# TensorE's transposes of x replaced by 32x32 block transposes on VectorE, with the delta made transposed, turned back, and added by GpSimd

## Chip, core and metric

The kernel runs on one core of a Trainium2 chip. The metric is the device time of one execution in microseconds (us), the median of several runs. Five engines with queues of their own take part: TensorE (PE; PEld is its weight load), VectorE (DVE), ScalarE (ACT), GpSimd (POOL) and SyncE (SP, which only issues transfers). Matmuls write PSUM. Everything is 32-bit float.

## What is computed

x is [8, 512, 2048]. A conditioning layer y = x W^T + b + 2 (x A_b) B_b, with a rank-16 adapter chosen per batch, feeds a layer with 8 experts of rank 16, of which each token takes the one with the largest router logit:

```python
base_out = jnp.einsum('bti,oi->bto', x, W) + b
A = lora_As[adapter_mapping]
Bm = lora_Bs[adapter_mapping]
lora_h = jnp.einsum('bti,bir->btr', x, A)
lora_out = jnp.einsum('btr,bro->bto', lora_h, Bm)
y = base_out + lora_out * 2.0
logits = jnp.einsum('bsd,ed->bse', y, route_w)
topk_v, topk_idx = jax.lax.top_k(logits, 1)
route_weight = one_hot(topk_idx[..., 0], 8) * topk_v
h = jnp.einsum('bsd,erd->bser', y, A_ffn)
wh = route_weight[..., None] * h
out = x + jnp.einsum('bser,eor->bso', wh, Bw)
```

## The kernel before

y is only read through 136 rows: 128 of the experts (8 times 16) and 8 of the router, gathered in `proj` (`pj` on chip). So the kernel folds W into them once, and y is never made: the heads of a token are hl = x (W^T proj + 2 A_b (B_b proj)) + bias proj.

First stage, the fold. W comes as eight slices of 256 columns over all 2048 rows (line 92, 2 MB each, SP's queue, three buffers), with the first tiles of x between them. For each block of 128 columns, 16 matmuls against `pj` are summed in PSUM (`pc`, line 150) and copied by ScalarE to `c_sb` (line 157). Between them come the bias row (`pb`, line 172) and the adapters, which GpSimd gathers (lines 128 and 135): `ad_b` is transposed on TensorE (line 163) and multiplied with `pj` (`pg`, line 189), and a masked copy per batch is kept in `gm`.

For each batch, `fold_adapter` makes m_b = c + 2 A_b (B_b proj): 16 matmuls of `ad_a` with `gm` over all 128 partitions (`pm`, line 217), and VectorE's adds to `c_sb` (line 224).

Token stage: 32 tiles of 128 tokens go through three stages, one tile apart. `stage_transpose` turns the tile's 16 blocks of 128x128 on TensorE (`pxT`, line 163), four to a PSUM bank, and ScalarE copies each bank to `xT` (line 164). `stage_route` multiplies xT with m_b (`ph`, line 243), and a chain of seven small VectorE instructions (lines 247 to 258) picks the expert and gives `wh`, the weighted heads. `stage_out` transposes wh (`pw`, line 269), ScalarE copies it (`whT`, line 271), and four matmuls of 512 columns with whT as the weights and `fb` (the experts' output matrices) moving give the delta in token order (`po`, line 274); VectorE adds each to the tile of x in place (line 275), and GpSimd's queue stores the tile (line 279, 1 MB, 128 partitions). SP's queue loads x six tiles ahead (line 86).

The order of each engine's work is the tile framework's scheduler's, within the dependences and the buffers of the pools. One f32 matmul appears in the profile as two matmul records; a transpose as one.

Of the kernel before, what the change touches and what calls it, by code (L numbers as in the profile page):

```python
# [9 lines left out]
F32 = mybir.dt.float32  # L10
# [8 lines left out]
def kernel(  # L19
# [12 lines left out]
    """out = x + ffn(cond(x)), both linear up to the choice of one expert.  # L32

    The FFN reads y = cond(x) through NP = E*R + E rows only (its A rows, then
    its router rows), gathered in proj [D, NP].  So the products are taken as
        hl = x @ (W^T proj + 2 A_b (B_b proj)) + bias @ proj
    with A_b, B_b the adapter of batch b: y itself is never needed.

      x [B, T, D]        itok [1, B]          w [DO, D]
      bias [128, DO/128], column c holds rows c*128...  # L40
      cond_a [SLOTS*R, D], cond_b [SLOTS*R, DO], row = slot*R + r
      proj [DO, NP]      ffn_b [E*R, D], row = e*R + r
    """
    nc = tc.nc
    P = 128
    B, T, D = x.shape
# [5 lines left out]
    NI = D // P  # L52
    NO = DO // P
    WS = 256
    NWS = D // WS
    TPB = T // P
    NT = B * TPB
    NN = D // 512
# [3 lines left out]
    wpool = ctx.enter_context(tc.tile_pool(name="wpool", bufs=3))  # L62
    xpool = ctx.enter_context(tc.tile_pool(name="xpool", bufs=6))
    xtpool = ctx.enter_context(tc.tile_pool(name="xtpool", bufs=2))
    mpool = ctx.enter_context(tc.tile_pool(name="mpool", bufs=2))
    small = ctx.enter_context(tc.tile_pool(name="small", bufs=3))
    ps_t = ctx.enter_context(tc.tile_pool(name="ps_t", bufs=2, space=bass.MemoryType.PSUM))
    ps_a = ctx.enter_context(tc.tile_pool(name="ps_a", bufs=3, space=bass.MemoryType.PSUM))
    ps_o = ctx.enter_context(tc.tile_pool(name="ps_o", bufs=3, space=bass.MemoryType.PSUM))

# [1 line left out]
    it_i = const.tile([P, B], I32, name="it_i")  # L72
    nc.gpsimd.dma_start(out=it_i, in_=itok.to_broadcast([P, B]))  # L73
    pj = const.tile([P, NO, NP], F32, name="pj")
    nc.scalar.dma_start(out=pj, in_=proj.rearrange("(c p) e -> p c e", p=P))
    bias_sb = const.tile([P, NO], F32, name="bias_sb")
    nc.scalar.dma_start(out=bias_sb, in_=bias)
    fb = const.tile([P, D], F32, name="fb")
    nc.scalar.dma_start(out=fb, in_=ffn_b)

    x_tiles = {}

    def load_x(t):
        xt = xpool.tile([P, D], F32, tag="x", name=f"x_{t}")
        b, k = divmod(t, TPB)
        nc.sync.dma_start(out=xt, in_=x[b, ts(k, P), :])
        x_tiles[t] = xt

    w_tiles = []
    for s in range(NWS):  # L90
        wt = wpool.tile([P, NO, WS], F32, tag="w", name=f"w_{s}")
        nc.sync.dma_start(
            out=wt, in_=w[:, ts(s, WS)].rearrange("(c p) i -> p c i", p=P)
        )
        w_tiles.append(wt)
        if s >= 2:
            load_x(s - 2)

# [1 line left out]
    ident = const.tile([P, P], F32, name="ident")  # L100
    make_identity(nc, ident)
    # own[p, b] = p - R*b, in [0, R) where row p = (b, r) belongs to batch b
# [9 lines left out]
    # rank[p, e] = E - e: the largest among equal logits is the first expert  # L112
# [14 lines left out]
    ad_b = const.tile([P, DO], F32, name="ad_b")  # L127
# [6 lines left out]
    ad_a = const.tile([P, D], F32, name="ad_a")  # L134
    nc.gpsimd.indirect_dma_start(  # L135
        out=ad_a,
# [3 lines left out]
    )  # L140

# [1 line left out]
    c_sb = const.tile([P, NI, NP], F32, name="c_sb")  # L143

    def fold_w(s):
        for k in range(WS // P):
            ic = s * (WS // P) + k
            pc = ps_a.tile([P, NP], F32, tag="acc", name=f"pc_{ic}")
            for oc in range(NO):
                nc.tensor.matmul(  # L150
                    pc,
                    w_tiles[s][:, oc, ts(k, P)],
                    pj[:, oc, :],
                    start=(oc == 0),
                    stop=(oc == NO - 1),
                )
            nc.scalar.copy(c_sb[:, ic, :], pc)  # L157

    def transpose_rows(dst, src, name, n):
        for g in range(n // 4):  # L160
            pt = ps_t.tile([P, 4, P], F32, tag="tr", name=f"{name}_{g}")
            for j in range(4):
                nc.tensor.transpose(pt[:, j, :], src[:, ts(4 * g + j, P)], ident)  # L163
            nc.scalar.copy(dst[:, 4 * g : 4 * g + 4, :], pt)  # L164

    for s in range(NWS - 2):
        fold_w(s)

    # bias @ proj on all partitions
    pb = ps_a.tile([1, NP], F32, tag="acc", name="pb")  # L170
    for oc in range(NO):
        nc.tensor.matmul(  # L172
            pb,
            bias_sb[:, oc : oc + 1],
            pj[:, oc, :],
            start=(oc == 0),
            stop=(oc == NO - 1),
        )
    c0 = const.tile([1, NP], F32, name="c0")
    nc.vector.tensor_copy(c0, pb)  # L180
    c0b = const.tile([P, NP], F32, name="c0b")
    nc.gpsimd.partition_broadcast(c0b, c0)  # L182

    # g[(b, r), e] = B_b proj, scaled, one masked copy per batch
    ad_bT = xtpool.tile([P, NO, P], F32, tag="xT", name="ad_bT")
    transpose_rows(ad_bT, ad_b, "pbT", NO)
    pg = ps_a.tile([P, NP], F32, tag="acc", name="pg")
    for oc in range(NO):
        nc.tensor.matmul(
            pg,  # L190
            ad_bT[:, oc, :],
            pj[:, oc, :],
            start=(oc == 0),
            stop=(oc == NO - 1),
        )
    g_sb = const.tile([P, NP], F32, name="g_sb")
    nc.vector.tensor_copy(g_sb, pg)
    gm = const.tile([P, B, NP], F32, name="gm")
    for b in range(B):
        nc.vector.tensor_scalar(  # L200
            gm[:, b, :], g_sb, mask[:, b : b + 1], COND_SCALING, ALU.mult, ALU.mult
        )

    for s in range(NWS - 2, NWS):
        fold_w(s)

# [1 line left out]
    m_tiles = {}  # L208
    GRP = 512 // NP

    def fold_adapter(b):
        m = mpool.tile([P, NI, NP], F32, tag="m", name=f"m_{b}")
        for i0 in range(0, NI, GRP):
            n = min(GRP, NI - i0)
            pm = ps_a.tile([P, GRP, NP], F32, tag="acc", name=f"pm_{b}_{i0}")
            for j in range(n):
                nc.tensor.matmul(  # L217
                    pm[:, j, :],
                    ad_a[:, ts(i0 + j, P)],
                    gm[:, b, :],  # L220
                    start=True,
                    stop=True,
                )
            nc.vector.tensor_tensor(  # L224
                m[:, i0 : i0 + n, :], c_sb[:, i0 : i0 + n, :], pm[:, :n, :], ALU.add
            )
        m_tiles[b] = m
# [54 lines left out]
    for t in range(NT + 2):  # L282
        if t < NT:
            stage_transpose(t)
# [56 lines left out]
```

## Time and profile before

| | |
|---|---|
| median of 3 runs (lowest, highest) | 433.1 us (432.74, 433.37) |
| span of the profiled execution, first to last instruction | 431.1 us |
| TensorE busy | 403.6 us, 94% of the span |
| VectorE, ScalarE, GpSimd busy | 163.4, 87.5, 21.4 us |
| transfers | 88.57 MB, mean 205 GB/s |

The profile has one execution. Its span is 2.0 us under the median. A row of the table of groups gives line, engine, operation, what is written and read, shape and count, then busy time in us and the mean of one in ns, and after the bar the idle time ahead of it with what ended it. A row of the table by stage gives a stretch, its length, the busy time of PE, PEld, DVE, ACT and POOL with counts, the granted clock of TensorE, the busy share of the transfer engines and GB/s. A row of the timeline gives start, duration, engine and line.

### The profile page before, as it was taken

How to read it: one execution, taken by the hardware profiler on the slowest of the kernel's cores; microseconds unless marked ns; L12 is line 12 of the kernel's file. 1: busy time of each engine (PE TensorE's matmuls, PEld its weight loads, DVE VectorE, ACT ScalarE, POOL GpSimd, SP SyncE). 2: the span in 40 equal slices, each digit the busy share in tenths (PEclk: the TensorE clock that was granted, in tenths of full speed). 3: DMA queues.
4: the chain of work that ended last, by engine and by line, in shares of the span. 5: the costliest groups of instructions: out<-in, count | busy, mean ns of one | idle time of the engine just before them, and what ended most of it. 6: DMA issues, size and time to landing. Idle time of an engine off the chain costs nothing.

```text
span 431.1 us, 6278 instructions
## 1 busy us (share of the span) xinstructions
PE 403.6 (94%) x2672; PEld 326.9 (76%) x2672; DVE 163.4 (38%) x420; ACT 87.5 (20%) x181; POOL 21.4 (5%) x44
## 2 busy tenths in 40 slices
PE   0589999999999999999999999999999999999993
PEld 0589998999777787779777877777787777777751
DVE  0100000121633453454554455544364336334562
ACT  1000011024222212312221222122303321322200
POOL 1200000000000000000000000000000000000000
PEclk9999999999999999999999999999999999999998
DMA  8999999100246553557265545554563565362224
GB/s 240 370 377 377 365 366 372 76 2 2 98 155 236 197 228 163 202 202 278 106 242 239 196 169 222 195 196 195 207 246 135 213 252 220 132 246 111 100 98 195
DMA packets 28429, 88.57 MB, mean 205 GB/s; under 512 B 1392, under 2 KB 19824, under 8 KB 19824
## 3 DMA queue, kind: packets, MB, share of 16 engines
q1 hardware_dynamic: 21120, 50.33, 33.3%
q0 software_dynamic: 4928, 35.66, 20.3%
q10 hardware_dynamic: 2352, 2.17, 1.6%
q8 instruction: 21, 0.34, 0.3%
q14 instruction: 8, 0.07, 0.0%
HBM read 54.60 MB, written 33.55 MB: 204 GB/s over the span
## 4 chain that ended last, share of the span: by engine, by line
issue 93%; POOL 4%; POOLq 0%; DVE 0%
POOL out_dram L279 4%; POOLq L279 0%; POOL ad_b L128 0%; POOL ad_a L135 0%; POOLq L337 0%; POOL c0b L182 0%; POOL ident masks.py:199 0%; POOL ident masks.py:197 0%; DVE it_f L122 0%; DVE row_f L124 0%; DVE rank L116 0%; DVE row_i L126 0%; DVE mask L111 0%; POOL it_i L73 0%; POOL own_i L104 0%
## 5 line engine op out<-in xcount | busy, mean ns | idle before, releaser
L243 PE MATMUL ph<-m,xT 128*128 128x136 f32 x1024 | 129.5, 279 | 0.0
L243 PEld LDWEIGHTS ph<-m,xT 128*128 128x128 f32 x1024 | 123.3, 190 | 0.5 <-issue 0.5
L274 PE MATMUL po<-fb,whT 128*128 128x512 f32 x256 | 118.4, 605 | 0.8 <-ACT whT L271 0.8
L164 ACT COPY xT<-pxT 128x512 f32<-128x512 f32 x128 | 71.2, 587 | 148.0 <-PE pxT L163 147.6
L275 DVE TENSOR_TENSOR x<-x,po 128x512 f32<-128x512 f32 x128 | 87.7, 685 | 13.4 <-PE po L274 12.3
L274 PEld LDWEIGHTS po<-fb,whT 128*128 128x128 f32 x256 | 46.0, 189 | 51.7 <-issue 27.7
L150 PE MATMUL pc<-pj,w 128*128 128x136 f32 x512 | 63.2, 286 | 18.4 <-DMA pj<-in_proj_dram 16.0
L150 PEld LDWEIGHTS pc<-pj,w 128*128 128x128 f32 x512 | 62.2, 196 | 19.1 <-DMA pj<-in_proj_dram 16.0
L163 PE MATMUL pxT<-ident,x 128*128 128x128 f32 x512 | 72.7, 277 | 0.9 <-ACT xT L164 0.2
L163 PEld LDWEIGHTS pxT<-ident,x 128*128 128x128 f32 x512 | 57.6, 140 | 19.8 <-issue 11.6
L247 DVE TENSOR_TENSOR hl<-ph,c0b 128x136 f32<-128x136 f32 x32 | 9.6, 300 | 151.0 <-PE ph L243 151.0
L279 POOL DMA_DIRECT2D out_dram<-x x32 | 17.2, 538 | 335.9 <-DVE x L275 335.9
L217 PEld LDWEIGHTS pm<-gm,ad_a 128*128 128x128 f32 x256 | 31.3, 190 | 3.3 <-issue 3.3
L217 PE MATMUL pm<-gm,ad_a 128*128 128x136 f32 x256 | 32.1, 279 | 0.0
L224 DVE TENSOR_TENSOR m<-c_sb,pm 128x408 f32<-128x408 f32 (+1 forms) x48 | 23.8, 529 | 15.6 <-PE pm L217 13.6
L271 ACT COPY whT<-pw 128x128 f32<-128x128 f32 x32 | 8.5, 265 | 101.2 <-PE pw L269 101.2
L180 DVE COPY c<-pb 1x136 f32<-1x136 f32 x1 | 0.3, 288 | 56.3 <-PE pb L172 56.3
L157 ACT COPY c_sb<-pc 128x136 f32<-128x136 f32 x16 | 4.4, 272 | 70.7 <-PE pc L150 70.7
L258 DVE TENSOR_TENSOR wh<-hl,rw 128x128 f32<-128x128 f32 x32 | 9.4, 293 | 1.1
L256 DVE TENSOR_SCALAR rw<-rank,win,top 128x8 f32<-128x8 f32 x32 | 9.3, 291 | 1.2
L269 PE MATMUL pw<-ident,wh 128*128 128x128 f32 x32 | 8.7, 273 | 0.0
L251 DVE TENSOR_SCALAR key<-hl,top 128x8 f32<-128x8 f32 x32 | 7.4, 231 | 1.1
(36 smaller groups left out, 49.8 us busy)
## 6 DMA issues: line engine op xcount, KB each, us to landing
x<-in_x_dram SPq DMA_DIRECT2D x32, 1024.0 KB, 4.8
out_dram<-x POOLq DMA_DIRECT2D x32, 1024.0 KB, 4.1
w<-in_w_dram SPq DMA_DIRECT2D x8, 2048.0 KB, 14.4
pj<-in_proj_dram ACTq DMA_DIRECT2D x1, 1088.0 KB, 15.2
fb<-in_ffn_b_dram ACTq DMA_DIRECT2D x1, 1024.0 KB, 13.1
bias_sb<-in_bias_dram ACTq DMA_DIRECT2D x1, 8.0 KB, 15.1
it_i<-in_itok_dram POOLq DMA_DIRECT2D x1, 4.0 KB, 6.3
ad_b<-in_cond_b_dram,row_i POOLq DMA_INDIRECT x1, 8.3
```

The lines of the kernel that those rows point to most:

```text
L150: nc.tensor.matmul(pc, w_tiles[s][:, oc, ts(k, P)], pj[:, oc, :], start=(oc == 0), stop=(oc == NO - 1),)
L163: nc.tensor.transpose(pt[:, j, :], src[:, ts(4 * g + j, P)], ident)
L164: nc.scalar.copy(dst[:, 4 * g : 4 * g + 4, :], pt)
L217: nc.tensor.matmul(pm[:, j, :], ad_a[:, ts(i0 + j, P)], gm[:, b, :], start=True, stop=True,)
L224: nc.vector.tensor_tensor(m[:, i0 : i0 + n, :], c_sb[:, i0 : i0 + n, :], pm[:, :n, :], ALU.add)
L243: nc.tensor.matmul(ph, xT[:, ic, :], m[:, ic, :], start=(ic == 0), stop=(ic == NI - 1))
L247: nc.vector.tensor_tensor(hl, ph, c0b, ALU.add)
L256: nc.vector.tensor_scalar(rw, rank, win, top, ALU.is_equal, ALU.mult)
L258: nc.vector.tensor_tensor(wh.rearrange("p (e r) -> p e r", r=R), hl[:, :ER].rearrange("p (e r) -> p e r", r=R), rw.unsqueeze(2).to_broadca ...
L274: nc.tensor.matmul(po, whT, fb[:, ts(n, 512)], start=True, stop=True)
L275: nc.vector.tensor_tensor(xt[:, ts(n, 512)], xt[:, ts(n, 512)], po, ALU.add)
L279: nc.gpsimd.dma_start(out=out[b, ts(k, P), :], in_=xt)
```

## The change

The tokens go in units of 256, in pairs of batches b and b+4. A unit of x lies on chip as [128, 8, 512]: partition (i, t) holds, for token t of each of eight groups of 32, the i-th quarter of the features. Each unit is loaded and stored in four pieces of 32 partitions, by SP and ScalarE in and by SP and GpSimd out. VectorE transposes it in 32x32 blocks straight from SBUF (`turn_x`), which leaves 128 features on the partitions and 128 tokens along each row; TensorE's transposes of x and ScalarE's copies of them go. `W`, `ad_a` and `fb` are put in the same order of features by copies (`chunked`) on ScalarE or GpSimd.

The heads and the choice of the expert stay. The delta is made with blocks of `fb` as weights and whT (256 tokens) moving, so it comes out with features on the partitions (`pd`); VectorE turns it back in 32x32 blocks from PSUM to `dl`, and GpSimd adds dl to x.

W comes in 16 row chunks of 1 MB; all of c is summed at once over the chunks in six PSUM banks. The first two chunks of pj are loaded ahead of the others. The adapters of two batches are folded together, each with the 64 partitions of its half. The order of instructions is that of the program (`manual_schedule`).

```diff
-    wpool = ctx.enter_context(tc.tile_pool(name="wpool", bufs=3))
-    xpool = ctx.enter_context(tc.tile_pool(name="xpool", bufs=6))
-    xtpool = ctx.enter_context(tc.tile_pool(name="xtpool", bufs=2))
...
+    DQ = D // NQ
+    U = 256
+    UPB = T // U
+    NU = B * UPB
+    TPU = U // P
+    NG = U // Q
+    GJ = 4
+    PH = P // 2
+    HB = B // 2
...
+    cpool = ctx.enter_context(tc.tile_pool(name="cpool", bufs=6))
+    rpool = ctx.enter_context(tc.tile_pool(name="rpool", bufs=4))
+    xpool = ctx.enter_context(tc.tile_pool(name="xpool", bufs=5))
+    dpool = ctx.enter_context(tc.tile_pool(name="dpool", bufs=2))
+    small = ctx.enter_context(tc.tile_pool(name="small", bufs=2))
+    ps_s = ctx.enter_context(tc.tile_pool(name="ps_s", bufs=2, space=bass.MemoryType.PSUM))
+    def chunked(copy, dst, src):
+        copy(
+            dst.rearrange("p j (i a) -> p j i a", a=Q),
+            src.rearrange("p (i j a) -> p j i a", i=NQ, a=Q),
+        )
+    ctx.enter_context(tc.manual_schedule())
...
+    def load_w(oc):
+        wt = rpool.tile([P, D], F32, tag="r", name=f"w_{oc}")
+        nc.sync.dma_start(out=wt, in_=w[ts(oc, P), :])
+        w_tiles.append(wt)
+    units = [UPB * (b + h * HB) + k for b in range(HB) for h in range(2) for k in range(UPB)]
+    x_tiles = {}
+    def rows_of(dram, u):
+        b, k = divmod(u, UPB)
+        return dram[b, ts(k, U), :].rearrange("(g t) (i d) -> i t g d", t=Q, i=NQ)
+    def load_x(u):
+        xt = xpool.tile([P, NG, DQ], F32, tag="x", name=f"x_{u}")
+        src = rows_of(x, u)
+        for i, eng in ((0, nc.sync), (2, nc.scalar), (1, nc.sync), (3, nc.scalar)):
+            eng.dma_start(out=xt[ts(i, Q)], in_=src[i])
+        x_tiles[u] = xt
+    nc.scalar.dma_start(out=pj[:, :2], in_=proj_v[:, :2])
+    load_w(0)
+    nc.scalar.dma_start(out=pj[:, 2:], in_=proj_v[:, 2:])
+    nc.scalar.dma_start(out=bias_sb, in_=bias)
+    for oc in range(1, 4):
+        load_w(oc)
...
+    raw = [xpool.tile([P, 2, D], F32, tag="x", name=f"raw_{k}") for k in range(2)]
+    ad_b = raw[0][:, 0, :]
...
+    ad_ar = raw[0][:, 1, :]
...
+    ad_a = const.tile([P, NJ, P], F32, name="ad_a")
+    chunked(nc.gpsimd.tensor_copy, ad_a, ad_ar)
...
+    c_sb = cpool.tile([P, NJ, NP], F32, tag="c", name="c_sb")
+    GRP = 512 // NP
+    groups = [(j0, min(GRP, NJ - j0)) for j0 in range(0, NJ, GRP)]
...
+    with tc.tile_pool(name="ps_c", bufs=len(groups), space=bass.MemoryType.PSUM) as ps_c:
+        pcs = [
+            ps_c.tile([P, GRP, NP], F32, tag="pc", name=f"pc_{j0}") for j0, n in groups
+        ]
+        def fold_w(oc):
+            wv = dpool.tile([P, NJ, P], F32, tag="d", name=f"wv_{oc}")
+            chunked(nc.scalar.copy, wv, w_tiles[oc])
+            for pc, (j0, n) in zip(pcs, groups):
+                for k in range(n):
+                    nc.tensor.matmul(
+                        pc[:, k, :],
+                        wv[:, j0 + k, :],
+                        pj[:, oc, :],
+                        start=(oc == 0 and k == 0),
+                        stop=(oc == NO - 1),
+                        skip_group_check=True,
+                    )
+                if oc == NO - 1:
+                    nc.scalar.copy(c_sb[:, j0 : j0 + n, :], pc[:, :n, :])
...
+        for oc in range(NO):
+            fold_w(oc)
+            if oc + 4 < NO:
+                load_w(oc + 4)
+            if oc == 2:
+                fbr = raw[1][:, 0, :]
+                nc.scalar.dma_start(out=fbr, in_=ffn_b)
+                chunked(nc.gpsimd.tensor_copy, fb, fbr)
+            if oc in (3, 6, 9):
+                load_x(units[oc // 3 - 1])
+            if oc == 7:
+                fold_bias()
+            if oc in (8, 9, 10, 11):
+                turn_adapters(oc - 8)
+            if oc == 12:
+                project_adapters()
+                load_x(units[3])
+    ps_m = ctx.enter_context(tc.tile_pool(name="ps_m", bufs=2, space=bass.MemoryType.PSUM))
+    ps_d = ctx.enter_context(tc.tile_pool(name="ps_d", bufs=2, space=bass.MemoryType.PSUM))
...
+    def fold_adapters(b):
+        pair = (b, b + HB)
+        for bb in pair:
+            m_tiles[bb] = cpool.tile([P, NJ, NP], F32, tag="c", name=f"m_{bb}")
+        for j0, n in groups:
+            pms = [
+                ps_m.tile([P, GRP, NP], F32, tag="m", name=f"pm_{bb}_{j0}") for bb in pair
+            ]
+            for k in range(n):
+                for h, bb in enumerate(pair):
+                    nc.tensor.matmul(
+                        pms[h][:, k, :],
+                        ad_a[ts(h, PH), j0 + k, :],
+                        gm[ts(h, PH), bb, :],
+                        start=True,
+                        stop=True,
+                    )
+            for h, bb in enumerate(pair):
+                nc.vector.tensor_tensor(
+                    m_tiles[bb][:, j0 : j0 + n, :],
+                    c_sb[:, j0 : j0 + n, :],
+                    pms[h][:, :n, :],
+                    ALU.add,
+                )
...
+    def turn_x(u, t):
+        xT = rpool.tile([P, NJ, P], F32, tag="r", name=f"xT_{u}_{t}")
+        nc.vector.transpose(
+            xT.rearrange("p j (g t) -> p g j t", t=Q),
+            x_tiles[u][:, ts(t, NQ), :].rearrange("p g (j a) -> p g j a", a=Q),
+        )
+        xT_tiles[u, t] = xT
+    def heads(u, t):
+        xT = xT_tiles.pop((u, t))
+        m = m_tiles[u // UPB]
+        ph = ps_s.tile([P, NP], F32, tag="s", name=f"ph_{u}_{t}")
+        for j in range(NJ):
+            nc.tensor.matmul(
+                ph, xT[:, j, :], m[:, j, :], start=(j == 0), stop=(j == NJ - 1)
+            )
...
+    def turn_heads(u):
+        pw = ps_s.tile([P, TPU, P], F32, tag="s", name=f"pw_{u}")
+        for t in range(TPU):
+            nc.tensor.transpose(pw[:, t, :], wh_tiles.pop((u, t)), ident)
+        whT = small.tile([P, U], F32, tag="whT", name=f"whT_{u}")
+        nc.scalar.copy(whT.rearrange("p (t q) -> p t q", q=P), pw)
+        whT_tiles[u] = whT
+    def delta(u, j0):
+        pd = ps_d.tile([P, GJ, U], F32, tag="d", name=f"pd_{u}_{j0}")
+        for k in range(GJ):
+            nc.tensor.matmul(pd[:, k, :], fb[:, j0 + k, :], whT_tiles[u], start=True, stop=True)
+        dl = dpool.tile([P, NG, GJ * Q], F32, tag="d", name=f"dl_{u}_{j0}")
+        nc.vector.transpose(
+            dl.rearrange("p g (k a) -> p k g a", a=Q),
+            pd.rearrange("p k (g t) -> p k g t", t=Q),
+        )
+        xs = x_tiles[u][:, :, ds(j0 * Q, GJ * Q)]
+        nc.gpsimd.tensor_tensor(xs, xs, dl, ALU.add)
+    def store(u):
+        xt = x_tiles.pop(u)
+        dst = rows_of(out, u)
+        for i, eng in ((0, nc.sync), (2, nc.gpsimd), (1, nc.sync), (3, nc.gpsimd)):
+            eng.dma_start(out=dst[i], in_=xt[ts(i, Q)])
+    fold_adapters(0)
+    for t in range(TPU):
+        turn_x(units[0], t)
+    for n in range(NU + 1):
+        u = units[n] if n < NU else None
+        v = units[n - 1] if n else None
+        w_ = units[n + 1] if n + 1 < NU else None
+        if u is not None:
+            heads(u, 0)
+        if v is not None:
+            delta(v, 0)
+            delta(v, GJ)
+        if w_ is not None:
+            turn_x(w_, 0)
+        if u is not None:
+            heads(u, 1)
+        if v is not None:
+            delta(v, 2 * GJ)
+            delta(v, 3 * GJ)
+            store(v)
+            if n + 3 < NU:
+                load_x(units[n + 3])
+        if w_ is not None:
+            turn_x(w_, 1)
+        if u is not None:
+            turn_heads(u)
+            if n % (2 * UPB) == 2 * UPB - 2 and n // (2 * UPB) + 1 < HB:
+                fold_adapters(n // (2 * UPB) + 1)
```

## The prediction

> **What bounds the kernel now.** I read the shares of busy time first, then the slices for clock and transfers, then the table by stage, the groups, and the timeline where a rate was needed.
>
> ```profile
> PE 403.6 (94%) x2672; PEld 326.9 (76%) x2672; DVE 163.4 (38%) x420; ACT 87.5 (20%) x181; POOL 21.4 (5%) x44
> ...
> PEclk9999999999999999999999999999999999999998
> ...
> GB/s 240 370 377 377 365 366 372 76 2 2 98 155 236 197 228 163 202 202 278 106 242 239 196 169 222 195 196 195 207 246 135 213 252 220 132 246 111 100 98 195
> ```
> ```profile
> 200.00:300.00 100.00, 99.84 (x627) 77.39 (x628) 47.01 (x120) 24.65 (x50) 4.78 (x9) 1.00 0.52 197
> ```
> TensorE is busy 94% of the span at full clock, and in the token stage (200 to 300 us) 99.84 of 100 us, while VectorE does 47, ScalarE 25, GpSimd 5 and the transfers run at half their share. So the token stage is as long as TensorE's list of instructions. In the first 75 us the transfers run at their top, 365 to 377 GB/s.
>
> ```profile
> L243 PE MATMUL ph<-m,xT 128*128 128x136 f32 x1024 | 129.5, 279 | 0.0
> L274 PE MATMUL po<-fb,whT 128*128 128x512 f32 x256 | 118.4, 605 | 0.8 <-ACT whT L271 0.8
> L164 ACT COPY xT<-pxT 128x512 f32<-128x512 f32 x128 | 71.2, 587 | 148.0 <-PE pxT L163 147.6
> L275 DVE TENSOR_TENSOR x<-x,po 128x512 f32<-128x512 f32 x128 | 87.7, 685 | 13.4 <-PE po L274 12.3
> L150 PE MATMUL pc<-pj,w 128*128 128x136 f32 x512 | 63.2, 286 | 18.4 <-DMA pj<-in_proj_dram 16.0
> L163 PE MATMUL pxT<-ident,x 128*128 128x128 f32 x512 | 72.7, 277 | 0.9 <-ACT xT L164 0.2
> L217 PE MATMUL pm<-gm,ad_a 128*128 128x136 f32 x256 | 32.1, 279 | 0.0
> L224 DVE TENSOR_TENSOR m<-c_sb,pm 128x408 f32<-128x408 f32 (+1 forms) x48 | 23.8, 529 | 15.6 <-PE pm L217 13.6
> ```
> The transposes of x are 72.7 us of TensorE, heads 129.5, the delta 118.4. Two records stand for one f32 product, one for a transpose. Means of single matmuls overlap, so I take the spacing from long runs:
>
> ```profile
> 75.78 14.99 PE L150 MATMUL pc<-pj,w 128*128 128x136 f32 x128
> ...
> 416.98 0.69 DVE L275 TENSOR_TENSOR x<-x,po 128x512 f32<-128x512 f32 x1 [0.16 <-PE po L274]
> ...
> 417.83 0.69 DVE L275 TENSOR_TENSOR x<-x,po 128x512 f32<-128x512 f32 x1
> ...
> 424.75 0.53 POOL L279 DMA_DIRECT2D out_dram<-x  x1 [3.69 <-DVE x L275]
> ```
> 128 records of 136 columns take 15.0 us: 0.116 us each. Two records of 512 columns are 0.85 apart: 0.43 each. A straight line gives 0.116 + 0.313*120/376 = 0.216 for 256 columns. From the last store's issue at 424.75 to the span's end at 431.1 is 6.4 us for 1 MB.
>
> **The change, part by part.** One iteration of the new loop is a unit of 256 tokens.
>
> TensorE per unit: heads 2*32*0.116 = 7.4; delta 16 products of 256 columns, 32*0.216 = 6.9 (the same columns, so no gain); two transposes of wh 0.3. Sum 14.6 us. Before, 256 tokens took two tiles of (423.7-94.2)/32 = 10.3, or 20.6. The 72.7 us of transposes is most of the difference. The adapter product has 64 rows per matmul in two row groups: 64 records a fold, 7.4 us if they run in turn, 3.7 if they pair; VectorE's 12 adds (10*0.577 + 2*0.29 = 6.4) and two buffers pace it either way, so I take 6.4 a fold.
>
> VectorE per unit loses eight adds of 0.685 and gains six block transposes. No transpose of VectorE is in the trace; the nearest rows are its adds: 128x512 in 0.685 and 128x408 in 0.577, that is 0.152 + N*1.04 ns. So 2048 elements take 2.29 and 1024 take 1.22. Lower bound: half the slope (1.2 and 0.7). Upper: twice the slope, if a 32-bit block is filled and emptied in turn (4.4 and 2.3). The row's slope is taken, since a transpose reads one stream where the add reads two. Per unit: 2*2.29 + 4*1.22 + two chains of small instructions at 1.81 (102.75 to 104.56 on the timeline) = 13.1 us, against TensorE's 14.6. Drawn out, it fits: transpose of x(t=1) ends 3.4 us into the next iteration, the next chain starts at 3.9. Slack is about 0.5 us, so anything that lengthens VectorE shows.
>
> GpSimd per unit: four adds of 1024. Nearest row: GpSimd's 128x128 select, 0.28 us, 2.2 ns an element, so 2.25 each, 9.0, plus two store issues at 0.54 to 1. It is hidden under 14.6; the cover ends at about 3.3 us an add. [...]
>
> [...] VectorE's chain waits for nobody on GpSimd in the trace, since GpSimd only issued transfers. [...]
>
> Transfers: 2.1 MB in and out per unit, each in four pieces of 32 partitions with 2 KB runs, on SP and ScalarE in, SP and GpSimd out. The trace shows 128-partition transfers alone: up to 377 GB/s with 1 KB runs, so 4.2 MB in 11.3 us, hidden. [...] On ScalarE each load waits until the stores from its buffer have landed, and the copy of whT is queued behind it; the stores have 12.5 us, and the copy a further 3.7 (heads t=0), before TensorE waits. SP's loads queue behind its stores, two units ahead of use.
>
> W by rows: the 512 records stay. W arrives 1 MB at a time in place of 2, and two chunks of pj go ahead, so the first product need not wait for all of pj (16.0 us now): bounds 9 and 16, I take 12. Each chunk gets a ScalarE copy of 2048 elements: from 128x512 in 0.587 and 128x128 in 0.265, 1.9 us, beside 3.7 of TensorE on two buffers: hidden after the first. GpSimd's re-ordering of ad_a and fb (4.5 us each by the select's rate) is long done when used. By the last chunk 27 MB have to be in, 74 us at 370 GB/s, about when TensorE wants it: I add 2.
>
> Sum, in us of the span: first product 12; W 59.4, bias 3.7, adapters 2.2 + 3.7: 81; transfers 83. The m adds, then the transpose of x behind them on VectorE, then the first unit without a partner (heads, chain, transpose, chain, exposed): 83 + 6.4 + 2.3 + 3.7 + 1.8 + 2.3 + 1.8 brings steady state at 101. 15 units*14.6 = 219, three folds 19, locks 4.5: 343.5. Last unit: previous adds and store issues, then GpSimd's four adds: 14. Store of 2 MB after it: 6.4 + 2.8 to 5 for the second MB, 10.5. Total 368. The profiled span of 431.1 stands 2.0 below the median 433.1, so 370.
>
> **Rivals.** [...]
>
> [...]
>
> *Slower: VectorE's transposes at half rate.* Place: six transposes a unit on VectorE's queue. At 2.08 ns an element VectorE takes 8192*2.08 + 6*0.152 + 3.6 = 21.6 a unit, 7.0 over TensorE: 370 + 16*7 - 4 (lock margin gone) = about 478; VectorE paces TensorE. The point: 433 leaves 63/15.5 = 4.1 more, 18.7 a unit, 1.73 ns an element. For: no row shows a 32-bit transpose, nor one from PSUM. Against: the adds hold 1.04 with two streams, one from PSUM.
>
> **How the numbers follow.** Within 0.2% is what a measurement of this kernel can't tell from no change. TensorE's list sets the loop: 0.46, 370 (own range 355 to 385). Transfers 0.24, 398. GpSimd or port 0.12, 395. VectorE at half rate 0.18, 478. The first three lie below 433 but for 0.02 of their upper ends; of that 0.01 within 0.2%. Faster 0.80, same 0.01, slower 0.19. The range 352 to 412 holds the first three.
>
> **What would show it.** Right: no pxT group; TensorE idle under 5% from 105 to 340 us; xT transposes near 2.29 and dl near 1.22 on VectorE; GpSimd adds near 2.25; delta spacing 0.216. [...]

## The result, and the profile after

The changed kernel takes 439.25 us (median of 4 runs, 436.82 to 440.82) against 433.06 for the kernel before: a ratio of 1.0137, interval 1.0111 to 1.0163. It is slower by 1.4%, where the forecast was 370 us, 14.6% less than before. The profiled execution took 436.82 us with a span of 435.0. In the runs below an execution over 1.5% above the fastest of its kernel counts as slow: the medians include these, the ratios (save that of e5) leave them out, and the profile of e2, of which eight executions in 19 are slow, is of a slow one and is not read.

The profile of the changed kernel, for the lines shown of before: busy shares, then clock and rate by slices.

```profile
PE 358.9 (83%) x2416; PEld 332.2 (76%) x2416; DVE 228.3 (52%) x388; ACT 42.1 (10%) x43; POOL 176.4 (41%) x110
...
PEclk9999999999579996799999759999976999999975
...
GB/s 258 400 322 277 252 296 284 266 305 53 0 1 98 2 203 240 267 62 154 227 293 286 237 269 85 129 231 292 283 233 294 87 128 226 299 202 121 129 196 152
```

TensorE works 45 us less than before and stands still 76 us in place of 28. The clock, at 9 throughout before, has four dips and a lower end. Its table by stage, for the same 100 us as before:

```profile
200.00:300.00 100.00, 94.14 (x606) 86.71 (x605) 75.39 (x123) 1.86 (x5) 57.31 (x33) 0.93 0.90 225
```

In the token stage TensorE is still nearly full. The groups of the changed kernel:

```profile
L350 POOL TENSOR_TENSOR x<-x,dl 128x1024 f32<-128x1024 f32 x64 | 149.6, 2360 | 189.4 <-DVE dl L345 187.0
L307 PE MATMUL ph<-m,xT 128*128 128x136 f32 x1024 | 131.9, 290 | 2.7 <-DVE xT L296 2.7
L343 PE MATMUL pd<-whT,fb 128*128 128x256 f32 x512 | 116.2, 380 | 3.6 <-ACT whT L336 3.6
L345 DVE STREAM_TRANSPOSE dl<-pd 128x1024 f32<-128x1024 f32 x64 | 80.0, 1250 | 24.1 <-PE pd L343 13.5
L189 PE MATMUL pc<-pj,wv 128*128 128x136 f32 x512 | 63.9, 287 | 32.4 <-ACT wv L82 32.4
L296 DVE STREAM_TRANSPOSE xT<-x 128x2048 f32<-128x2048 f32 x32 | 72.7, 2273 | 0.0
L274 PE MATMUL pm<-gm,ad_a 64*128 64x136 f32 x256 | 43.1, 416 | 14.2 <-DVE m L282 13.6
```

The transposes of x are gone from TensorE, and every new instruction has about the length forecast. The new idle time is before the products of W (L189, 32.4 us, waiting for ScalarE's copies) and inside the adapters' folds (L274, waiting for VectorE's adds; its mean rose from 279 to 416 ns, where the clock dips, as shown under e6).

The timeline of TensorE at the start shows where the 32.4 us lie. In brackets is the idle time ahead of the run of instructions, with what ended it.

```profile
21.61 28.72 PE L189 MATMUL pc<-pj,wv 128*128 128x136 f32 x224 [21.61 <-ACT wv L82]
...
62.76 0.60 PE L220 MATMUL pbT<-ident,raw 128*128 128x128 f32 x4
65.83 3.97 PE L189 MATMUL pc<-pj,wv 128*128 128x136 f32 x32 [2.47 <-ACT wv L82]
...
94.00 11.28 PE L189 MATMUL pc<-pj,wv 128*128 128x136 f32 x96
105.86 0.97 PE L274 MATMUL pm<-gm,ad_a 64*128 64x136 f32 x12 [0.58 <-issue]
...
120.78 10.10 PE L307 MATMUL ph<-m,xT 128*128 128x136 f32 x64 [2.68 <-DVE xT L296]
```

First product at 21.61, fold stage to 105.3, then the first unit; the loop runs from 133.2. The wait of 2.47 us comes four times: ScalarE's copy of `pbT` (L221) waits for TensorE's transposes, and the copy of the next chunk of W stands behind it in ScalarE's queue. ScalarE's own timeline says why the start is late:

```profile
1.21 0.49 ACTq L120 DMA_DIRECT2D pj<-in_proj_dram  x1
1.74 16.61 ACTq L121 DMA_DIRECT2D bias_sb<-in_bias_dram  x1
18.37 1.28 ACT L82 ACT_TABLE_LOAD   x1 [18.37 <-issue]
19.66 3.70 ACT L82 COPY wv<-w 128x2048 f32<-128x2048 f32 x2
...
92.15 1.90 ACT L82 COPY wv<-w 128x2048 f32<-128x2048 f32 x1 [3.51 <-DMA w<-in_w_dram]
```

The bias is 8 KB, but its issue, third in ScalarE's queue, held ScalarE for 16.61 us, with the first copy of W behind it. The last line bears on the end of the stage: the copy of the last chunk but one waited for W itself until 92.15 and ended at 94.05, just as TensorE came to it at 94.00.

### The profile page after: what moved, and what is told of

Same layout as the page of the kernel before. It is cut to its first block, busy times and chain, and to the rows that moved or that the text cites. A ratio compares the mean times of both kernels' runs of the same rounds, so it can differ in the third digit from the quotient of the medians.

```text
span 435.0 us, 5824 instructions
## 1 busy us (share of the span) xinstructions
PE 358.9 (83%) x2416; PEld 332.2 (76%) x2416; DVE 228.3 (52%) x388; ACT 42.1 (10%) x43; POOL 176.4 (41%) x110
## 4 chain that ended last, share of the span: by engine, by line
PE 56%; DMA 12%; DVE 10%; POOL 7%; ACT 3%; issue 3%; ACTq 1%; POOLq 0%; SPq 0%; DVEq 0%
PE ph L307 20%; PE pd L343 15%; PE pc L189 10%; DMA out_dram<-x 9%; PE pm L274 8%; POOL x L350 7%; DMA x<-in_x_dram 3%; DVE m L282 3%; ACT wv L82 3%; DVE xT L296 3%; DVE dl L345 2%; PE pb L204 1%; PE pg L227 1%; ACTq L115 1%; POOL out_dram L356 1%
## 5 line engine op out<-in xcount | busy, mean ns | idle before, releaser
L350 POOL TENSOR_TENSOR x<-x,dl 128x1024 f32<-128x1024 f32 x64 | 149.6, 2360 | 189.4 <-DVE dl L345 187.0
L343 PE MATMUL pd<-whT,fb 128*128 128x256 f32 x512 | 116.2, 380 | 3.6 <-ACT whT L336 3.6
L343 PEld LDWEIGHTS pd<-whT,fb 128*128 128x128 f32 x512 | 94.9, 190 | 16.6 <-ACT whT L336 4.9
L345 DVE STREAM_TRANSPOSE dl<-pd 128x1024 f32<-128x1024 f32 x64 | 80.0, 1250 | 24.1 <-PE pd L343 13.5
L189 PE MATMUL pc<-pj,wv 128*128 128x136 f32 x512 | 63.9, 287 | 32.4 <-ACT wv L82 32.4
L189 PEld LDWEIGHTS pc<-pj,wv 128*128 128x128 f32 x512 | 62.4, 196 | 33.8 <-ACT wv L82 33.6
L296 DVE STREAM_TRANSPOSE xT<-x 128x2048 f32<-128x2048 f32 x32 | 72.7, 2273 | 0.0
L274 PE MATMUL pm<-gm,ad_a 64*128 64x136 f32 x256 | 43.1, 416 | 14.2 <-DVE m L282 13.6
L274 PEld LDWEIGHTS pm<-gm,ad_a 64*128 64x128 f32 x256 | 35.3, 280 | 21.5 <-DVE m L282 20.2
L82 ACT COPY wv<-w 128x2048 f32<-128x2048 f32 x16 | 30.3, 1899 | 29.3 <-PE pc L189 11.1
## 6 DMA issues: line engine op xcount, KB each, us to landing
pj<-in_proj_dram ACTq DMA_DIRECT2D x1, 952.0 KB, 22.2
```

Of the source, the lines that this page charges most:

```text
L82: copy(dst.rearrange("p j (i a) -> p j i a", a=Q), src.rearrange("p (i j a) -> p j i a", i=NQ, a=Q),)
L189: nc.tensor.matmul(pc[:, k, :], wv[:, j0 + k, :], pj[:, oc, :], start=(oc == 0 and k == 0), stop=(oc == NO - 1), skip_group_check=True,)
L274: nc.tensor.matmul(pms[h][:, k, :], ad_a[ts(h, PH), j0 + k, :], gm[ts(h, PH), bb, :], start=True, stop=True,)
L296: nc.vector.transpose(xT.rearrange("p j (g t) -> p g j t", t=Q), x_tiles[u][:, ts(t, NQ), :].rearrange("p g (j a) -> p g j a", a=Q),)
L343: nc.tensor.matmul(pd[:, k, :], fb[:, j0 + k, :], whT_tiles[u], start=True, stop=True)
L345: nc.vector.transpose(dl.rearrange("p g (k a) -> p k g a", a=Q), pd.rearrange("p k (g t) -> p k g t", t=Q),)
```

## The experiments

Two theories were set against each other. A: the time went to the order of queues and to buffers (bias and pbT in ScalarE's queue, two buffers in the fold). B: it went to the transfers of x in pieces of 32 partitions. The medians in the order of running, each against runs of the kernel before on the same chip:

| run | median, us | ratio to before, interval | end of fold stage, us |
|---|---|---|---|
| after | 439.25 | 1.0137 (1.0111 to 1.0163) | 105.3 |
| e1_bias_pool | 436.42 | 1.0089 (1.0057 to 1.0120) | 105.1 |
| e2_pbt_dve | 437.72 | 1.0033 (1.0008 to 1.0058) | not read |
| e3_fold_full | 421.89 | 0.9762 (0.9701 to 0.9823) | 104.4 |
| e4_full_width | 429.13 | 0.9908 (0.9892 to 0.9925) | 103.8 |
| e5_pj_first | 439.84 | 1.0175 (1.0121 to 1.0228) | 105.8 |
| e6_fold_3buf | 404.27 | 0.9306 (0.9261 to 0.9351) | 108.9 |
| e7_all | 399.29 | 0.9177 (0.9123 to 0.9232) | 100.0 |
| e8_all_full_width | 373.22 | 0.8608 (0.8571 to 0.8645) | 84.3 |
| e9_by_groups | 687.3 | 1.5903 (1.5800 to 1.6005) | not read |
| e10_early_turn | 681.04 | 1.5713 (1.5686 to 1.5739) | not read |
| e11_x_later | 380.53 | 0.8760 (0.8729 to 0.8791) | 89.0 |

### The start: e1_bias_pool and e5_pj_first

```diff
-    nc.scalar.dma_start(out=bias_sb, in_=bias)
+    nc.gpsimd.dma_start(out=bias_sb, in_=bias)
```

> Only the load of bias_sb moves from ScalarE's queue to GpSimd's. Theory A (queues): ScalarE stood 16.6 us in the issue of that load, so its table load and first W copy came late; now the first W product starts at 10 to 13 us instead of 21.6. The second part of pj still lands near 23 us, so chunk 2 waits for it, and the total falls by 3 to 8 us from 437-439. Theory B (transfers in quarter pieces set the fold stage, which had its transfer engines at full share from 21 to 97 us): the first product starts earlier, but the last W chunk lands when it did, and the total falls by less than 2 us.

TensorE's timeline in e1:

```profile
9.94 9.39 PE L189 MATMUL pc<-pj,wv 128*128 128x136 f32 x64 [9.94 <-DMA pj<-in_proj_dram]
31.14 23.87 PE L189 MATMUL pc<-pj,wv 128*128 128x136 f32 x192 [11.80 <-DMA pj<-in_proj_dram]
```

The first product came at 9.94, and then TensorE stood for the second part of `pj`, 952 KB in runs of 544 bytes, which landed 29.8 us after its issue while W went past it in rows of 8 KB. The median fell by 2.8 us (2.1 by the ratios), between B's under 2 and A's 3 to 8, and the stage ended where it had, at 105.1. So e5 also put `pj` whole at the head of SP's queue:

```diff
-    nc.scalar.dma_start(out=pj[:, :2], in_=proj_v[:, :2])
+    nc.sync.dma_start(out=pj, in_=proj_v)
     load_w(0)
-    nc.scalar.dma_start(out=pj[:, 2:], in_=proj_v[:, 2:])
```

> The bias load on GpSimd's queue, as before, and the whole of pj in one load on SP's queue ahead of W's first chunk. If the late pj was the second half of the slow start (theory A): first W product at about 11 to 13 us (pj's 1.1 MB at 250 to 300 GB/s takes 4 us, then W), no wait of 11.8 us for pj after the second chunk, and the fold stage ends 6 to 10 us earlier, at 95 to 99: a median 6 to 10 us under the kernel after, about 430. If the transfers with quarter pieces of x set the end of the fold stage (theory B): the first product is early, but TensorE later waits for W's copies by as much, the stage ends at 103 to 105, and the median stays within 3 us of 436.

`pj` now landed in time and the first product came at 11.86. It brought nothing (its executions run from 434.66 to 442.33 us, those of e1 from 434.06 to 438.35): new waits of 1.57, 0.18 and 5.53 us for the copies of W, then the same four of 2.47, and the last run of products again starts at 94.47.

```profile
48.61 5.41 PE L188 MATMUL pc<-pj,wv 128*128 128x136 f32 x32 [5.53 <-ACT wv L82]
...
94.47 11.28 PE L188 MATMUL pc<-pj,wv 128*128 128x136 f32 x96
```

This is theory B's reading, though its numbers (103 to 105, and within 3 us of 436) are narrowly missed: a start 10 us earlier does not end the stage earlier.

### pbT: e2_pbt_dve

```diff
-            nc.scalar.copy(ad_bT[:, 4 * g : 4 * g + 4, :], pt)
+            nc.vector.tensor_copy(ad_bT[:, 4 * g : 4 * g + 4, :], pt)
```

> Only the four copies of the transposed adapter blocks (pbT) move from ScalarE to VectorE. Theory A (queues): each of them stood ahead of the next W copy on ScalarE and waited for TensorE, 2.47 us of TensorE idle four times; these go, and the total falls by 8 to 10 us. Theory B (transfers): the idle time comes back as waits of the W copy for W itself, and the total falls by less than 3 us.

By the ratios it gained 1.0% (1.0137 to 1.0033), 4.5 us, less than the four waits (9.9) and between A's 8 to 10 and B's under 3.

### The transfers alone: e4_full_width

```diff
-        return dram[b, ts(k, U), :].rearrange("(g t) (i d) -> i t g d", t=Q, i=NQ)
+        return dram[b, ts(k, U), :].rearrange("(p r) (i d) -> i p r d", r=2, i=NQ)
...
-            eng.dma_start(out=xt[ts(i, Q)], in_=src[i])
+            eng.dma_start(out=xt.rearrange("p (r i) d -> i p r d", i=NQ)[i], in_=src[i])
```

> x is loaded and stored in pieces of 128 partitions, two runs of 2 KB on each, with the same bytes, sizes, queues and number of transfers as before; tokens and features then lie where the transposes don't expect them, so the values differ from the reference's and only the time is read. Theory A (queues): transfer engines' share falls from 0.9-1.0 to near 0.6 in the loop, the waits of whT behind loads and of ScalarE for a load in the fold stage go, and the total falls by 5 to 12 us. Theory B (transfers in quarter pieces set the time): the fold stage shortens by 10 us or more and the loop too, in all 20 us or more.

It gained 10.1 us, in A's range. The table by stage from 21 to 97 us, in the changed kernel and then in e4:

```profile
21.00:97.00 76.00, 64.59 (x522) 62.11 (x523) 2.28 (x10) 28.98 (x19) 4.26 (x3) 1.00 1.01 286
21.00:97.00 76.00, 65.53 (x535) 63.26 (x536) 2.28 (x10) 29.40 (x20) 4.25 (x3) 1.00 0.82 297
```

The transfers' share falls from 1.01 to 0.82, yet the fold stage ends at 103.8, because the waits of 2.47 us and the late start are still there. Between the two profiled spans, 6.5 us apart, 4.0 lie from the last unit's delta on, 1.5 in the fold stage and 1.5 in the loop, where TensorE's waits for `whT` fell from 3.6 us to 0.5; the stretch between the stage and the loop took 0.6 more.

### The fold of the adapters: e3_fold_full and e6_fold_3buf

In e3 each batch is folded by itself over all 128 partitions, one buffer for one group:

```diff
-            for k in range(n):
-                for h, bb in enumerate(pair):
-                    nc.tensor.matmul(pms[h][:, k, :], ad_a[ts(h, PH), j0 + k, :], gm[ts(h, PH), bb, :], start=True, stop=True)
+        for bb in pair:
+            for j0, n in groups:
+                for k in range(n):
+                    nc.tensor.matmul(pm[:, k, :], ad_a[:, j0 + k, :], gm[:, bb, :], start=True, stop=True)
```

> Only the fold of the adapters changes: batch by batch over all 128 partitions, so that a group takes one of the two PSUM buffers and TensorE and VectorE can alternate; the pairing of the two halves is given up. Theory A (both buffers taken by one pair, TensorE and VectorE in turn, and the clock dropping to 0.5 in these stretches): a fold and the slow heads behind it cost 9 to 10 us instead of 16.5, and the first one 8 instead of 12; the clock stays at 1.0, and the total falls by 22 to 28 us. Theory B (it is the pairing that saves and VectorE's backlog that makes the wait): without pairs TensorE's work doubles from 3.7 to 7.4 us a fold, and the total falls by less than 8 us or rises.

It gained 17.4 us: a fold took 12.9 us (158.0 to 170.9) with twice TensorE's work. That is neither A's 22 to 28 nor B's under 8, and the clock fell for a time here too (0.58 on the mean of 162 to 166). It does not yet say whether the pairing or the buffers were at fault. e6 keeps the pairs and gives them buffers:

```diff
-    ps_m = ctx.enter_context(tc.tile_pool(name="ps_m", bufs=2, space=bass.MemoryType.PSUM))
-    ps_d = ctx.enter_context(tc.tile_pool(name="ps_d", bufs=2, space=bass.MemoryType.PSUM))
+    ps_d = ctx.enter_context(tc.tile_pool(name="ps_d", bufs=3, space=bass.MemoryType.PSUM))
...
-            pms = [
-                ps_m.tile([P, GRP, NP], F32, tag="m", name=f"pm_{bb}_{j0}") for bb in pair
-            ]
+            pm2 = ps_d.tile([P, 2, 512], F32, tag="d", name=f"pm_{b}_{j0}")
+            pms = [
+                pm2[:, h, : GRP * NP].rearrange("p (k e) -> p k e", e=NP) for h in range(2)
+            ]
```

> The adapters of two batches are folded in pairs of 64 rows as in the kernel after, but both tiles of a group are one buffer of the delta's pool, which gets three buffers of two banks in place of two, so three groups are in flight in place of one. If the number of buffers made the fold slow (A): a fold takes 8 to 9 us in place of about 15 (six groups paced by VectorE's two adds of 0.53, 6.4 us, and a wait of 2 to 3 ahead), TensorE and VectorE overlap, and the heads behind run at 3.7 to 4.3: 7 to 9 us less a fold, 21 to 27 over three and a few at the first, a median of 410 to 418, under the version with 128 rows (421.9). If the pairing itself is slow (the 64-row matmuls don't overlap, or lower the clock): a fold stays at 12 us or more and the median at 425 or above.

The timeline of one fold in the changed kernel:

```profile
162.41 0.97 PE L274 MATMUL pm<-gm,ad_a 64*128 64x136 f32 x12
165.74 1.03 DVE L282 TENSOR_TENSOR m<-c_sb,pm 128x408 f32<-128x408 f32 x2
166.33 2.21 PE L274 MATMUL pm<-gm,ad_a 64*128 64x136 f32 x12 [2.95 <-DVE m L282]
168.14 1.07 DVE L282 TENSOR_TENSOR m<-c_sb,pm 128x408 f32<-128x408 f32 x2 [1.38 <-PE pm L274]
168.78 2.21 PE L274 MATMUL pm<-gm,ad_a 64*128 64x136 f32 x12 [0.23 <-DVE m L282]
```

and in e6:

```profile
159.12 2.36 PE L274 MATMUL pm<-gm,ad_a 64*128 64x136 f32 x36
162.44 5.36 DVE L282 TENSOR_TENSOR m<-c_sb,pm 128x408 f32<-128x408 f32 x12
163.62 2.46 PE L274 MATMUL pm<-gm,ad_a 64*128 64x136 f32 x28 [2.15 <-DVE m L282]
166.01 3.97 PE L307 MATMUL ph<-m,xT 128*128 128x136 f32 x32
```

In the first, each engine waits for the other: a group's two tiles take both buffers, so the next group starts only when VectorE frees one, and VectorE waits 1.38 us for each group. In the second VectorE's adds run in one piece. A fold takes 6.9 us (159.12 to 166.01) in place of 15.0 (162.41 to 177.36). The clock has a part in it: in the changed kernel twelve records took 0.97 us in the first group and 2.21 in the next, and the table by stage says

```profile
168.00:180.00 12.00, 11.06 (x55) 9.53 (x53) 4.87 (x10) 0.00 (x0) 0.09 (x1) 0.50 1.05 291
```

a granted clock of 0.50 through the fold and into the heads behind it. In e6 it was 1.00 over the fold shown, though TensorE waited 2.15 us there too. In e1, which has the changed kernel's two buffers, twelve records took 1.45 us in place of 2.21 in four groups of the fold ahead of the loop (107 to 115), and a group came every 1.91 us in place of 2.45. By that, an estimate, the clock makes 3.7 of the 10.1 us by which a fold and the heads behind it exceed the forecast (four groups at 0.54, and 1.5 in the heads); the rest is the turns and the wait of 2.95 us for VectorE ahead of them. The median fell by 35.0 us, more than A's 21 to 27. From span to span, the loop (first heads of its steady part to the last delta) went from 273.5 to 243.9 us; the stages around it changed by 3 together. e6 also gives the delta a third buffer; the three folds and their heads make 28 of the 29.6 us in the loop, so little is left for it. So buffers, not pairing, set the fold.

### Together: e7_all and e8_all_full_width

e7 has the edits of e5, e2 and e6; e8 adds those of e4.

> The bias load on GpSimd's queue, pj ahead of W, the copies of pbT on VectorE and the paired fold with three buffers, together. If the parts add (A): 439 less 6 to 10 (start) less 4 to 5 (pbT, now that W is in) less 21 to 27 (folds): 397 to 408, under the kernel before by 6 to 8%. If the fold stage is set by the transfers (B): the start and pbT bring 3 us together, and the median is 409 to 416.

> The same, with x and out moved in pieces of all 128 partitions with the same bytes, queues and number of pieces; the values of the output are other than the reference's. It tells what the pieces of 32 partitions still cost once queues and buffers are mended. A: in the kernel after it was 9.5 us, of which the fold stage gave 1.5 and the units and the tail the rest; so 6 to 9 under the run before it (390 to 402), from whT no longer late and a shorter tail. B: the fold stage ends 6 us or more earlier than with quarter pieces, and the median is 12 or more us under it.

TensorE's timeline of the fold stage in e7 and then in e8:

```profile
47.15 6.97 PE L188 MATMUL pc<-pj,wv 128*128 128x136 f32 x32 [4.45 <-ACT wv L82]
...
90.64 9.35 PE L188 MATMUL pc<-pj,wv 128*128 128x136 f32 x64 [2.83 <-ACT wv L82]
```
```profile
11.97 21.31 PE L188 MATMUL pc<-pj,wv 128*128 128x136 f32 x160 [11.97 <-ACT wv L82]
33.80 11.39 PE L188 MATMUL pc<-pj,wv 128*128 128x136 f32 x96 [0.51 <-ACT wv L82]
...
73.02 11.28 PE L188 MATMUL pc<-pj,wv 128*128 128x136 f32 x96
```

and the copies' group in e7, whose waits are for the transfers now:

```profile
L82 ACT COPY wv<-w 128x2048 f32<-128x2048 f32 x16 | 30.4, 1898 | 63.5 <-DMA w<-in_w_dram 47.2
```

With the queues in order, e7 gained 5 us over e6 and its fold stage still ended at 100.0: W came late behind x's pieces. With full width it ends at 84.3, and the median falls by 26.1 us more. For the fold stage this is B's outcome in both runs; e7's median lies in A's range only because e6 alone had given more than A expected. The four corners are therefore there: neither mended 105.3, queues alone 100.0, width alone 103.8, both 84.3. (Where its code was that of the changed kernel, the stage ended at 104.4 in e3 and at 108.9 in e6, so of the first three only the 100.0 stands apart.) Two causes with nearly the same due time covered each other; mending one showed next to nothing. The other 8 us between e7 and e8 are 4 in the loop (246.9 to 242.5) and 4 behind the last delta (28.3 to 24.3).

### With the kernel's own layout: e9_by_groups, e10_early_turn, e11_x_later

e8's layout of x is not the one that the kernel needs. e9 keeps the needed layout and all 128 partitions. It has e7's mends, and a unit goes in eight pieces in place of four, in and out; a piece is one group of 32 tokens over all partitions:

```diff
-        for i, eng in ((0, nc.sync), (2, nc.scalar), (1, nc.sync), (3, nc.scalar)):
-            eng.dma_start(out=xt[ts(i, Q)], in_=src[i])
+        for g in range(NG):
+            eng = nc.scalar if g % 2 else nc.sync
+            eng.dma_start(out=xt[:, g], in_=src[:, :, g])
```

> The four mends of the run with all of them, and x and out moved in eight pieces a unit in place of four: one piece is a group of 32 tokens over all 128 partitions (256 KB, runs of 2 KB), on the same queues, so that x lies as the kernel needs it. If the 32 partitions of a piece were what held the transfers down (A): transfers at 400 GB/s in the fold stage, its end at 84 to 87 us, whT not late, and a median of 371 to 380. If more and smaller pieces cost as much as the width gives (B; GpSimd has four issues of 0.6 to 0.8 us more a unit, SP four): 388 to 400.

> As the run before it, with two changes of order: VectorE turns the first unit's two halves ahead of the first fold of adapters, and in the last unit VectorE makes two of the four adds of dl to x that GpSimd makes. Expected from the trace of the run with all mends and full width: the wait of 4.0 us of TensorE for xT behind the first fold goes, and the adds of the last unit, which ended 7.4 us after its last delta, end 3 to 4 us earlier: 6 to 8 us less than the run before it, 364 to 372. If VectorE's and GpSimd's adds exclude each other at the end, the second gain is under 1 us: 368 to 376.

Both took over 680 us; neither theory had it. A stretch of e9's table by stage:

```profile
340.00:350.00 10.00, 7.85 (x78) 7.14 (x77) 9.42 (x16) 0.00 (x0) 7.42 (x6) 0.89 0.29 101
```

The transfers ran at 101 GB/s here, a quarter of e8's 409 (20 to 60 us), and the transfer engines at a share of 0.29; of the seven stretches of 10 us from 300 to 370, five are like this one (0.26 to 0.29) and two stand at about 0.7, with 160 to 166 GB/s. What made them so slow is not shown: no view here counts the engines of one piece, and the greater number of pieces was not tried apart. e10 came out 6 us under e9, about what its changes of order were to give.

e11 goes back to pieces of 32 partitions, in e7, and moves x out of W's way: one unit among W's chunks, three behind the last, with GpSimd's queue in place of ScalarE's; the first unit is turned ahead of the first fold, and VectorE makes two of the last four adds.

```diff
-            if oc in (3, 6, 9):
-                load_x(units[oc // 3 - 1])
+            if oc in (3, 11, 12):
+                load_x(units[max(oc - 10, 0)], nc.gpsimd)
...
-                load_x(units[3])
+            if oc == 14:
+                load_x(units[3], nc.gpsimd)
...
+    for t in range(TPU):
+        turn_x(units[0], t)
     fold_adapters(0)
-    for t in range(TPU):
-        turn_x(units[0], t)
```

> The run with all four mends (399.3), quarter pieces as in the kernel after, with three changes of order: of the first four units of x only the first is loaded among W's chunks, the others behind W's last chunk, into the stretch of 100 to 130 us in which that run moved 36 GB/s; these loads go to SP and GpSimd in place of SP and ScalarE; VectorE turns the first unit ahead of the first fold of adapters, and makes two of the last unit's four adds. If what the quarter pieces cost is W's chunks that come late behind them (A): no wait for W, fold stage ended at 82 to 86 in place of 100, 4 us less before the first heads, 3 us less at the end, and a loop about 4 us longer than with full width: 372 to 380. If x is then late for the first units (B), TensorE waits for it after the fold by as much as it saved: 388 to 400.

TensorE's timeline in e11:

```profile
11.92 32.57 PE L188 MATMUL pc<-pj,wv 128*128 128x136 f32 x256 [11.92 <-ACT wv L82]
...
85.00 3.97 PE L188 MATMUL pc<-pj,wv 128*128 128x136 f32 x32 [1.42 <-ACT wv L82]
89.56 4.75 PE L274 MATMUL pm<-gm,ad_a 64*128 64x136 f32 x64 [0.58 <-issue]
94.23 7.68 PE L307 MATMUL ph<-m,xT 128*128 128x136 f32 x64
```

380.53 us (377.62 to 385.70), 12.4% under the kernel before: A's outcome, just past its upper end of 380. The stage ends at 89.0, past A's 82 to 86, with waits for copies of W left, and the first heads follow at the full rate with no wait for `xT`. Against e7's span the 22.0 us are 11.0 in the fold stage, 6.6 between it and the loop, 2.0 in the loop, 2.3 at the end. TensorE never waits for x, so B's cost did not come.

## Why the prediction was wrong

The sum can be laid beside the spans of three runs, cut at the same points (first product, end of the fold stage, start of the second unit's heads, start of the last unit's delta, end):

| stage | forecast | after | e8 | e11 |
|---|---|---|---|---|
| to the first product | 12 | 21.6 | 12.0 | 11.9 |
| fold stage | 71 | 83.7 | 72.3 | 77.1 |
| to the loop | 18 | 27.9 | 21.9 | 15.4 |
| loop, with three folds | 242.5 | 273.5 | 242.5 | 244.9 |
| last unit and store | 24.5 | 28.2 | 24.3 | 25.9 |
| span | 368 | 435.0 | 372.9 | 375.2 |

The forecast fits e8, with two buffers more in the fold, two queues re-ordered and transfers of full width; it left out what these three removed. That it meets e8's loop to the tenth is luck: the 4.5 us set aside for locks (VectorE held up by GpSimd's adds) were not needed, and stood in for longer folds (22 us for the three, against 19) and small waits.

**Right.** The mechanism: the transposes leave TensorE and VectorE carries them, a unit of the loop without a fold takes 14.6 us (at 193.4 to 208.0 TensorE is busy for all of 14.60), xT 2273 ns against 2.29 us, dl 1250 against 1.22, GpSimd's adds 2360 against 2.25, ScalarE's copies 1899 against 1.9. VectorE at half rate, the only slower outcome it named (0.18), is excluded: the transposes run at 1.11 ns an element, and the kernel is slower for other reasons. No run shows the 4.5 us for locks: in the changed kernel the chain's `wh` took 291 to 294 ns in all 32 cases, against 293 before; what was seen are the last adds of e11, outside the loop. GpSimd's adds had ended just before the chain's steps with two inputs from SBUF (in the unit from 193.4: at 197.80 against 198.17, and at 205.17 against 205.33).

**"two buffers pace it either way, so I take 6.4 a fold".** This is the step that failed most. 6.4 us is VectorE's share, and stands alone only if TensorE fills the next group meanwhile. With both buffers in one group the two engines take turns and their times add up. A fold cost 15.0, and its heads another 1.5 at half clock: (15.0 + 1.5 - 6.4)*3 = 30 of the 31 us by which the loop exceeded its forecast; the 4.5 not used for locks covers the late `whT` (3.6). The code had it: two buffers and two tiles a group. e6, with 6.9 a fold, shows it, though that this is so near 6.4 is partly chance: VectorE begins its adds 3.3 us into the fold, behind its transposes, TensorE waits 2.15 us for it, and the heads start while the last adds run.

**"first product 12".** I counted the bytes ahead of the product, not the instructions ahead of ScalarE's first copy. The issue of the bias's load has no term in the sum: 9.6 us. The trace of before had a hint of it, since the same load, second in that queue, held ScalarE there for 4.97 us, when nothing was waiting for it:

```profile
1.23 4.97 ACTq L77 DMA_DIRECT2D bias_sb<-in_bias_dram  x1
```

**"beside 3.7 of TensorE on two buffers: hidden after the first".** The copies' length was right, their place was not: TensorE waited four times 2.47 us for a copy of W queued behind one of `pbT`. These 9.9 us, and 0.9 behind an issue of x's loads on ScalarE, make 10.8 of the 12.7 us by which the fold stage exceeded its forecast. Taken away alone they would not have brought it in: W's own arrival stood close behind them (e7).

**"27 MB have to be in, 74 us at 370 GB/s".** The 370 came from whole-width transfers, and x's first four units come in quarters: 286 GB/s in the changed kernel from 21 to 97 us. At that rate 27 MB take 94 us. Alone this cost little, since the queues held the stage to the same time; it is what e5 and e7 ran into.

**"brings steady state at 101" and the tail.** To the loop it took 10 us more than forecast, of which e6's buffers gave back 7 (108.9 to 129.9 there) and turning the first unit ahead of the fold another 6 (e11). From the last unit's delta on it took 4 more, for the stores in quarters (28.2, against 24.3 at full width).

**"Transfers 0.24, 398".** This had the right resource and the wrong place. No run shows a term that gives the 398, nor one for the 395 of "GpSimd or port": the loop moved 225 GB/s at a share of 0.90 in the changed kernel and 259 at 1.00 in e7 (200 to 300 us), and GpSimd's adds took 2360 ns. The loop lost 3.6 us to late `whT`; the fold stage lost its time. Of the signs of being right, idle time of TensorE under 5% from 105 to 340 us failed (9%); none of them looked at the folds or the start.

## What to carry to other kernels

Cost a fold between two engines from the number of groups in flight, not from the number of buffers: two buffers taken by one group are one, and then the engines' times add (15.0 us a fold here, against 6.9 with three groups in flight). When two causes end a stage at nearly the same time, mending one shows next to nothing (100.0 and 103.8 from 105.3 here, and 84.3 with both), so try them together before dropping either. List for each engine's queue everything ahead of the instruction that starts a stage, loads of a few KB included (8 KB held ScalarE for 16.61 us).

## What was not expected of the hardware

- The issue of an 8 KB load behind two others held ScalarE for 16.61 us. With that load on GpSimd's queue the first product came at 9.94, and the hold passed to the next load on ScalarE's queue, that of `fb`:

```profile
15.73 10.19 ACTq L247 DMA_DIRECT2D raw<-in_ffn_b_dram  x1
```

Both holds ended 5 us before the second part of `pj`, ahead in the queue, had landed (18.4 and 23.4; 25.9 and 31.0). With `pj` landed, the issue of `fb` took 0.35 (the changed kernel, e3 and e4). So it goes with the load ahead, not with the bias; why was not tried.
- A load of 952 KB in 544-byte runs took 22.2 us to land (29.8 in e1) beside W's rows of 8 KB; ahead of W, all 1088 KB took 6.8 (e8). Why the share was so small is not settled here.
- TensorE's clock was 0.50 for 12 us in which it was busy for 11.06, with a pause of 0.23 in every 2.45 (the changed kernel, 168 to 180). In a fold of e7 it was 0.50 from 156 to 159 and 1.00 from 159.5 on. TensorE's wait ended at 155.66, the heads ran at the full rate from 159.13, 3.5 us later, and between them lie nothing but products of 64 rows and no pause:

```profile
155.66 3.54 PE L273 MATMUL pm<-gm,ad_a 64*128 64x136 f32 x28 [2.15 <-DVE m L281]
156.00:159.00 3.00, 3.00 (x28) 2.87 (x26) 2.71 (x7) 0.00 (x0) 0.85 (x2) 0.50 1.05 246
159.50:162.00 2.50, 2.50 (x24) 2.50 (x23) 0.76 (x3) 0.00 (x0) 0.00 (x0) 1.00 1.05 331
```

In folds of e8 and e11 the same 28 records took 3.50 us (from 139.84) and 3.47 (from 204.91), against 2.46 at a clock of 1.00 in e6, and the 32 of the heads behind them 3.97, as in e7. That the short pauses kept the clock down in the changed kernel is the author's estimate from these three folds: no run takes them away alone. What brings it down is open: it was at 0.50 behind the wait of 2.15 us here, and at 1.00 behind the same wait in the fold of e6 shown.
- Products with 64 rows in two halves go faster by the record: 12 in 0.97 us, 0.08 each, and 36 in 2.36 in e6, 0.066 each, against 0.116 for 128 rows, as if the halves overlapped.
- At the end of e11 VectorE's adds, with two inputs from SBUF, ran longer beside GpSimd's, by what was left of GpSimd's. VectorE's add of 1024 elements, started with GpSimd's, took 3.45 us: GpSimd's 2.36 and then 1.09. In the second pair it started 1.08 us after GpSimd's add of 2.34 and took 2.33, which is the rest of that add and 1.07.

```profile
354.36 2.36 POOL L351 TENSOR_TENSOR x<-x,dl 128x1024 f32<-128x1024 f32 x1
354.36 3.45 DVE L351 TENSOR_TENSOR x<-x,dl 128x1024 f32<-128x1024 f32 x1
```

The transposes, with one input, ran beside GpSimd's adds at their usual 1.25 and 2.27 (the changed kernel, from 162.37 and 163.54).
